# Weights of small blocks inverted by VectorE's reciprocal in place of ScalarE's Ln and Exp

## The chip, the cores and the metric

One core of a Trainium2 chip runs the whole program. The metric is device time in microseconds; the median of three runs of the kernel before is 5099.17 us (5098.44 to 5099.74). The profile was taken in one execution of its own, whose time stands in the table below. Engine names are those of the profile: PE (TensorE), DVE (VectorE), ACT (ScalarE), POOL (GpSimd), SP (SyncE, which issues the transfers).

## What is computed

Eight sequences of 512 tokens with 128 channels pass through two parts, all in float32. The first part, which the change touches, is one attention layer whose weights are not a softmax. For each of 16 heads of 8 channels the scores s = QK^T / sqrt(8) are taken over the causal positions, and a number lam is found for each row by four Newton steps so that the weights 1/(lam - s) sum to 1. Then the weights are taken once more, normalised, and applied to V:

```
lam = s_masked.max(-1) + 1.0
for _ in range(num_iter):                      # 4
    d = maximum(lam[..., None] - s, EPS)
    w = where(mask, 1 / d, 0.0)
    f = w.sum(-1) - 1.0
    fp = -where(mask, 1 / d**2, 0.0).sum(-1)
    lam = lam - f / fp
p = where(mask, 1 / maximum(lam[..., None] - s, EPS), 0.0)
o = (p / p.sum(-1, keepdims=True)) @ V
```

The second part is a stack of six layers with local attention and a feed-forward block each. Nothing in it is changed.

## The kernel before, in words

In the first part, a sequence (`b`) is cut into four row blocks of 128 queries (`rb` 0 to 3). Block `rb` sees W = 128 (rb + 1) keys. The 16 heads are taken in four quarters (`j` 0 to 3) of four heads; a quarter's scores for a block lie in one tile of 4W - 192 columns: 320, 832, 1344 and 1856 for rb 0 to 3. The columns hold four pieces, one for each 32 queries, with their own number of keys.

A loop over `work` takes two blocks at a time: (3, 0) of a sequence, then (2, 1) of it. Three such pairs are under way together. For the pair `nxt`, `scores` (L237) multiplies queries and keys on PE and stores the negated scores `ns` with their minimum through DVE (L253). For the pair `now`, `newton` (L283) makes one Newton step a round. For the pair `before`, which has its final lam, `attend_add` (L317) adds lam to the scores on POOL (L263, tile `da`), `attend_weigh` (L322) inverts the sum on ScalarE as Exp(-Ln(d)) in place (L324, L325), and `attend_sum` (L327) transposes the weights on PE (L338), masks them into SBUF on DVE (L341), multiplies by V on PE (L350) and copies the result out on DVE (L354). A loop of four rounds (`k`) inside does one quarter of `before` and of `nxt` and one Newton step of both blocks of `now` in each round.

A Newton step of a large block (W over 256) takes Ln with lam as bias for each piece (L297) and one Exp (L298) on ScalarE; for a small block POOL adds lam first (`add_lams`, L263, tile `df`) and one Ln (L293) and one Exp (L298) follow. DVE's statistics instruction (L300) gives means and spreads from which a chain of small DVE operations (L304 to L315, with a reciprocal of 16 columns in L313) makes the new lam. The next step of the same block waits for it.

The order of the instructions on each engine is set by a planner in the framework, which goes by its own cost of each operation, not by the source's order alone; each engine then works its queue off in that order. The tiles `da` rotate through three buffers; each of the score tiles `ns` of a block has a single buffer, so the next pair's scores wait until POOL has read the old ones. At the end of a pair `attend_end` (L362) divides by the sum of weights and applies the output weights, and once a sequence `normalized_T` (L88) and `project` (L190, with four copies in L198) prepare the next one. The second part has a reciprocal of 8 columns (L665) that is cited below.

Of the kernel before, what the change touches and what calls it, by code (L numbers as in the profile page):

```python
# [11 lines left out]
AF = mybir.ActivationFunctionType  # L12
# [4 lines left out]
P = 128  # L17
# [33 lines left out]
def tile_kernel(  # L51
# [18 lines left out]
    nc = tc.nc  # L70
# [38 lines left out]
    with ExitStack() as c1:  # L109
# [211 lines left out]

        def attend_weigh(t):  # L322
            d = t["d"]
            nc.scalar.activation(d, d, AF.Ln)  # L324
            nc.scalar.activation(d, d, AF.Exp, scale=-1.0)  # L325

        def attend_sum(t, d, j):  # L327

# [62 lines left out]
        for w in range(len(work) + 1):  # L391
            before, now, nxt = now, nxt, []
            if w + 1 < len(work):
                b, rbs = work[w + 1]
                nxt = [block(b, rb, proj) for rb in rbs]
            for t in now:
                first_lam(t)
            for k in range(NUM_ITER):
                if now:
                    add_lams(now[1])  # L400
                for u in range(2):
                    if before:
                        attend_add(before[u], k)
                    if nxt:
                        scores(nxt[u], k)
                    if now:
                        newton(now[u], k)
                    if ready:
                        attend_sum(*ready)
                        ready = None  # L410
                    if before:
                        attend_weigh(before[u])
                        ready = (before[u], before[u]["d"], k)
            if w + 2 < len(work) and work[w + 2][1][0] == 3:
                if ready:
                    attend_sum(*ready)
                    ready = None
                proj = project(work[w + 2][0])
# [412 lines left out]
    t = -1  # L831
# [100 lines left out]
```

## Time and profile before

| | |
|---|---|
| Time, median of 3 runs | 5099.17 us |
| Profiled execution, time / span | 5096.4 us / 5094.7 us |
| DVE busy | 4292.8 us (84%) |
| PE busy | 4212.5 us (83%) |
| ACT busy | 3544.0 us (70%) |
| POOL busy | 2982.7 us (59%) |
| First part (to about 1692 us): ACT, DVE, PE, POOL busy | 1492, 1404, 968, 751 us |
| L324 and L325, 320 columns, 32 each | 454 ns each |
| L324 and L325, 832 columns, 32 each | 884 and 886 ns each |

Busy time of an engine is the union of its instructions. Neighbouring instructions on DVE and ACT overlap by some tens of nanoseconds, since the next begins before the last one's result has been written; where an engine is never idle, the time from start to start is what an instruction costs. In the groups, a line gives the kernel line, engine, operation, the tile written and read, the shape, how often it ran, its busy time and mean duration, and the idle time of the engine before it with what ended it.

### The profile page before, as it was taken

How to read it: one execution, taken by the hardware profiler on the slowest of the kernel's cores; microseconds unless marked ns; L12 is line 12 of the kernel's file. 1: busy time of each engine (PE TensorE's matmuls, PEld its weight loads, DVE VectorE, ACT ScalarE, POOL GpSimd, SP SyncE). 2: the span in 40 equal slices, each digit the busy share in tenths (PEclk: the TensorE clock that was granted, in tenths of full speed). 3: DMA queues.
4: the chain of work that ended last, by engine and by line, in shares of the span. 5: the costliest groups of instructions: out<-in, count | busy, mean ns of one | idle time of the engine just before them, and what ended most of it. 6: DMA issues, size and time to landing. Idle time of an engine off the chain costs nothing.

```text
span 5094.7 us, 163374 instructions
## 1 busy us (share of the span) xinstructions
PE 4212.5 (83%) x67981; PEld 2491.9 (49%) x67981; DVE 4292.8 (84%) x11404; ACT 3544.0 (70%) x6314; POOL 2982.7 (59%) x3827
## 2 busy tenths in 40 slices
PE   4556566556554899999999999999999999999998
PEld 1223233223322555555555555565555555556555
DVE  7789888888887888888888888888888888888886
ACT  6889999999898566665666666656666566665664
POOL 2444434444445766666666666666666666666663
PEclk7667667667665999999999999999999999999999
DMA  0000000000001323232233222332223223233231
GB/s 9 1 5 1 5 5 1 5 3 3 3 1 26 72 58 73 61 76 64 56 73 72 65 67 58 74 75 56 69 58 81 68 55 72 61 76 73 62 75 47
DMA packets 273626, 237.61 MB, mean 47 GB/s; under 512 B 47056, under 2 KB 269048, under 8 KB 272888
## 3 DMA queue, kind: packets, MB, share of 16 engines
q1 hardware_dynamic: 272888, 227.16, 19.0%
q8 instruction: 538, 8.81, 0.8%
q14 instruction: 200, 1.64, 0.1%
HBM read 21.52 MB, written 4.19 MB: 5 GB/s over the span
## 4 chain that ended last, share of the span: by engine, by line
PE 43%; DVE 30%; ACT 19%; POOL 5%; issue 2%; SPq 0%; DMA 0%; ACTq 0%; POOLq 0%; DVEq 0%
PE m L552 9%; PE po L685 6%; DVE qr L568 5%; DVE stw L300 5%; DVE ss L558 5%; ACT d L297 5%; DVE qn L560 5%; PE pT L673 4%; PE acc L711 3%; ACT d L298 3%; PE ptq L619 3%; PE pv L588 3%; POOL da L263 2%; PE y L782 2%; PE gp L761 2%
## 5 line engine op out<-in xcount | busy, mean ns | idle before, releaser
L572 POOL TENSOR_TENSOR qn<-qn,qr 128x512 f32<-128x512 f32 x768 | 977.8, 1273 | 1047.4 <-DVE qr L568 827.2
L580 POOL TENSOR_TENSOR qn<-qn,ss 128x512 f32<-128x512 f32 x768 | 784.7, 1043 | 58.6 <-ACT ss L577 58.6
L558 DVE TENSOR_REDUCE ss<-sq 128x8 f32<-128x512 f32 x768 | 521.4, 679 | 351.0 <-ACT sq L557 351.0
L263 POOL TENSOR_TENSOR df<-ns,lam 128x32 f32<-128x32 f32 (+7 forms) x1024 | 396.9, 425 | 604.9 <-DVE lam L315 390.7
L552 PE MATMUL m<-wqkv,xs 128*128 128x512 f32 x1536 | 726.9, 596 | 2.0 <-ACT v L592 1.7
L297 ACT ACTIVATE d<-ns,lam 128x416 f32<-128x416 f32 (+7 forms) x1024 | 559.5, 615 | 64.9 <-DVE stw L300 27.5
L557 ACT ACTIVATE sq<-m 128x512 f32<-128x512 f32 x768 | 453.8, 597 | 187.4 <-PE m L552 184.7
L568 DVE TENSOR_TENSOR qr<-m,tab 128x256 f32<-128x256 f32 x1536 | 570.6, 412 | 0.0
L300 DVE BATCH_NORM_STATS2 stw<-d 128x6 f32<-128x416 f32 (+7 forms) x1024 | 514.6, 561 | 56.1 <-ACT d L298 55.7
L248 PE MATMUL s<-kn,qj 32*32 32x160 f32 (+15 forms) x4096 | 423.6, 491 | 151.4 <-DVE mn L253 136.6
L624 ACT COPY qT<-ptq 128x512 f32<-128x512 f32 x768 | 419.9, 579 | 175.1 <-PE ptq L619 175.1
L338 PE MATMUL dTp<-ident,da 128*128 128x128 f32 x1280 | 295.3, 371 | 294.8 <-issue 68.6
L560 DVE TENSOR_TENSOR qn<-m,tab 128x512 f32<-128x512 f32 x768 | 521.5, 679 | 0.0
L263 POOL TENSOR_TENSOR da<-ns,lam 128x416 f32<-128x416 f32 (+15 forms) x512 | 310.7, 639 | 319.3 <-PE dTp L338 252.5
L619 PEld LDWEIGHTS ptq<-ident,qn 128*128 128x128 f32 x3072 | 360.0, 141 | 210.4 <-issue 157.6
L685 PE MATMUL po<-v,prT 64*32 64x64 f32 x24576 | 389.3, 223 | 87.0 <-DVE pr L644 86.9
L588 PE MATMUL pv<-wqkv,xs 128*128 128x512 f32 x768 | 431.8, 644 | 4.9
L650 POOL TENSOR_TENSOR pr<-pr,nm 128x512 f32<-128x512 f32 x384 | 400.8, 1044 | 19.3 <-PE ptq L619 8.8
L711 PE MATMUL acc<-oT,wo 128*128 128x512 f32 x768 | 397.6, 599 | 14.9 <-ACT oT L705 14.9
L619 PE MATMUL ptq<-ident,qn 128*128 128x128 f32 x3072 | 399.3, 273 | 7.2 <-DVE qr L568 3.6
L338 PEld LDWEIGHTS dTp<-ident,da 128*128 128x128 f32 x1280 | 198.5, 186 | 422.3 <-issue 208.7
L685 PEld LDWEIGHTS po<-v,prT 64*32 64x32 f32 x24576 | 323.5, 105 | 166.5 <-DVE pr L644 136.5
(139 smaller groups left out, 8477.1 us busy)
## 6 DMA issues: line engine op xcount, KB each, us to landing
v<-v SPq DMA_DIRECT2D x1152, 128.0 KB
v<-v SPq DMA_DIRECT2D x384, 96.0 KB
v<-v SPq DMA_DIRECT2D x192, 64.0 KB
wqkv<-in_L_ffn_Wqkv_dram SPq DMA_DIRECT2D x24, 256.0 KB
wqkv<-in_L_ffn_Wqkv_dram SPq DMA_DIRECT2D x24, 128.0 KB
wo<-in_L_ffn_Wo_dram SPq DMA_DIRECT2D x12, 256.0 KB
xb<-in_L_attn_x_dram SPq DMA_DIRECT2D x8, 256.0 KB
x<-xb SPq DMA_DIRECT2D x8, 256.0 KB
```

Source lines behind the costliest of these rows:

```text
L263: nc.gpsimd.tensor_tensor(o, n, by.to_broadcast([P, keys(W, a)]), ALU.add)
L297: nc.scalar.activation(dv[a], nv[a], AF.Ln, bias=lam[:, c : c + 1])
L300: nc.vector.bn_stats(st[:, 4 * j + a].rearrange("p u k -> p (u k)"), dv[a])
L552: nc.tensor.matmul(m.rearrange("p h e -> p (h e)"), lhsT=lhsT, rhs=wqkv[:, t, :], start=True, stop=True,)
L558: nc.vector.tensor_reduce(ss[:, t, :], sq, axis=AX.X, op=ALU.add)
L560: nc.vector.tensor_tensor(qc, m, tab[:, 2 * t, c, :].unsqueeze(1).to_broadcast([P, HH, DHL]), ALU.mult)
L568: nc.vector.tensor_tensor(qr[:, :, u, :], mh[:, :, 1 - u, :], sw.unsqueeze(1).to_broadcast([P, HH, hd]), ALU.mult,)
L572: nc.gpsimd.tensor_tensor(qc, qc, qr.rearrange("p h u e -> p h (u e)"), ALU.add)
L580: nc.gpsimd.tensor_tensor(qc, qc, ss[:, t, :].unsqueeze(2).to_broadcast([P, HH, DHL]), ALU.mult)
L588: nc.tensor.matmul(pv, lhsT=lhsT, rhs=wqkv[:, 2, :], start=True, stop=True,)
L619: nc.tensor.transpose(pt[:, c * P : (c + 1) * P], g["qn"][t][:, c, 2 * p : 2 * p + 2, :].rearrange("p h e -> p (h e)"), ident,)
L685: nc.tensor.matmul(po[u * QB : (u + 1) * QB, e, c, :], lhsT=prT[rows, c, u * QB : (u + 1) * QB], rhs=g["v3"][rows, n, p * DHL : (p + 1) * ...
```

## The change

The blocks with W of at most 256 (rb 0 and 1) are inverted by one VectorE reciprocal of the whole quarter's tile, in place, instead of by ScalarE's Ln and Exp. Blocks 2 and 3 stay as they were, and so do all Newton steps. In the changed kernel's numbering the reciprocal is L325, and every later line moves down by three.

```
         def attend_weigh(t):
             d = t["d"]
-            nc.scalar.activation(d, d, AF.Ln)
-            nc.scalar.activation(d, d, AF.Exp, scale=-1.0)
+            if t["W"] <= 2 * P:
+                nc.vector.reciprocal(d, d)
+            else:
+                nc.scalar.activation(d, d, AF.Ln)
+                nc.scalar.activation(d, d, AF.Exp, scale=-1.0)
```

## The prediction

> **What bounds the kernel now.** I read the page's busy totals first, then busy time by stage, then groups by shape, and last the order of time on ScalarE and VectorE inside one iteration.
>
> ```profile
> span 5094.7 us, 163374 instructions
> PE 4212.5 (83%) x67981; PEld 2491.9 (49%) x67981; DVE 4292.8 (84%) x11404; ACT 3544.0 (70%) x6314; POOL 2982.7 (59%) x3827
> ...
> 629.00:830.00 201.00, 122.30 (x1040) 62.25 (x1040) 171.97 (x628) 184.78 (x268) 89.38 (x194) 0.67 0.01 4
> ...
> 0.00:1692.00 1692.00, 967.64 (x8370) 494.35 (x8370) 1404.33 (x5082) 1492.37 (x2161) 751.03 (x1642) 0.68 0.03 7
> ```
>
> The shares over the whole span mislead. The change is in the first part (to about 1692 us), and there ACT is busy 88% and DVE 83%; PE and POOL are at 57% and 44%. A window's line gives, after its length, PE, PEld, DVE, ACT and POOL. First_lam (L269) starts at 629.0 and 830.2: a batch takes 201.2 us. In the window 629 to 830 ACT is busy 184.8 us and DVE 172.0 us, so ACT leads with VectorE 13 us behind. Inside the batch:
>
> ```profile
> 659.20:684.30 25.10, 18.57 (x144) 7.78 (x143) 21.99 (x95) 22.81 (x32) 9.28 (x24) 0.67 0.00 1
> 684.30:707.50 23.20, 10.64 (x93) 5.91 (x93) 20.95 (x81) 22.79 (x32) 9.28 (x24) 0.61 0.00 1
> 727.50:773.80 46.30, 28.93 (x232) 15.58 (x232) 36.67 (x132) 36.89 (x56) 18.89 (x35) 0.65 0.05 12
> 773.80:797.20 23.40, 14.63 (x128) 7.27 (x129) 20.37 (x79) 22.29 (x31) 13.74 (x28) 0.69 0.00 1
> 797.20:818.20 21.00, 13.85 (x135) 6.18 (x137) 20.01 (x80) 21.00 (x32) 12.07 (x24) 0.69 0.00 1
> ```
>
> The first two windows are Newton iterations of row blocks 3 and 0, while blocks 2 and 1 of the batch before are weighed (call this stage A: its small block has 832 columns). The last two are iterations of blocks 2 and 1, with 3 and 0 being weighed (stage B, small block 320 columns). The middle one is the border, with the next batch's projection. An iteration is 21 to 25 us; ACT fills 91 to 100% of it, but DVE already fills 87 to 95%.
>
> **What goes.** ScalarE loses Ln (L324) and Exp (L325) of the small blocks, 32 of each at each size.
>
> ```profile
> 629.57 0.88 ACT L293 ACTIVATE df<-df 128x832 f32<-128x832 f32 x1
> 630.36 0.45 ACT L324 ACTIVATE da<-da 128x320 f32<-128x320 f32 x1
> 630.72 0.88 ACT L298 ACTIVATE df<-df 128x832 f32<-128x832 f32 x1
> ...
> L665 DVE RECIPROCAL rs<-rs 128x8 f32<-128x8 f32 x384 | 76.2, 199 | 8.3
> L313 DVE RECIPROCAL sw<-sw 128x16 f32<-128x16 f32 x128 | 30.5, 239 | 0.1
> ...
> 505.55 0.24 DVE L313 RECIPROCAL sw<-sw 128x16 f32<-128x16 f32 x1
> 505.71 0.20 DVE L300 BATCH_NORM_STATS2 stw<-df 128x6 f32<-128x96 f32 x1
> 505.83 0.17 DVE L314 TENSOR_TENSOR sw<-sw,sw 128x16 f32<-128x16 f32 x1
> 505.92 0.29 DVE L300 BATCH_NORM_STATS2 stw<-df 128x6 f32<-128x128 f32 x1
> ...
> 2015.21 0.20 DVE L665 RECIPROCAL rs<-rs 128x8 f32<-128x8 f32 x1
> 2015.33 0.64 DVE L693 TENSOR_TENSOR o<-po,rs 128x512 f32<-128x512 f32 x1
> ```
>
> Durations of neighbours overlap, so the cost on a busy engine is start to start: 832 columns take 630.36 - 629.57 = 0.79 us on ACT, 320 columns 630.72 - 630.36 = 0.36 us. ACT loses 2 x 0.79 = 1.58 us in each iteration of stage A and 0.72 us in each of stage B; over the kernel 32 x (1.58 + 0.72) = 73.6 us.
>
> **What comes.** VectorE gets 32 reciprocals of 320 and 32 of 832 columns. The trace has none that large, so I bound the slope. From 8 to 16 columns the duration goes from 199 to 239 ns, 5.0 ns a column; start to start it goes from 0.12 (2015.21 to 2015.33) to 0.16 us (505.55 to 505.71), also 5.0 at this rounding, and 4 where other instances show 0.15. I take 4.5 ns: 832 columns 0.155 + 816 x 4.5 ns = 3.83 us, 320 columns 0.155 + 304 x 4.5 ns = 1.52 us; 171 us over the kernel. Lower end: the slope of BATCH_NORM_STATS2 on this engine, (675 - 449) ns over 512 - 288 columns = 1.0 ns, giving 0.98 and 0.47 us. Upper end: L314 shows 0.09 us for 16 columns, so some 0.07 us is fixed; if a reciprocal had no more than 0.06 us fixed, 8 columns would cost 7.5 ns each: 6.3 and 2.5 us. The middle is nearest to the rows of the operation itself.
>
> The Trainium skill speaks against the change: "VectorE: DVE Perf Modes", section "First, the fixed hardware budget", says that Reciprocal is an iterative divide with a repeat count of 8. Read as 8 clocks of 0.96 GHz a column that is an estimate of 8.3 ns, about 7 us for 832 columns, and the sum would come out some 105 us higher than mine. The step between 8 and 16 columns, 0.04 us, is half of that, so the row decides.
>
> **What lies on the path.** In stage A the order of the changed kernel puts the 832 reciprocal on VectorE between the statistics (L300) of the third and of the fourth quarter of block 3. Behind it wait that fourth L300, the chain L304 to L315 and so lam; ScalarE's next four L297 wait for lam. Free VectorE time in such an iteration is 25.10 - 21.99 = 3.1 and 23.20 - 20.95 = 2.25 us, and 3.83 us must fit. Even with no wait left it grows by 0.7 and 1.6 us; ACT, at 22.8 - 1.58 = 21.2, is no longer the limit. Taking 1.15 for each of 4 iterations: +4.6 us a stage.
> At the border two 320 reciprocals come close together, among the normalization and the qj copies (L101, L198). VectorE is free 9.6 of 46.3 us there, but these stretches are a chain over PE, ACT and DVE; of 3.04 us I put half on the path (ends 0 and 3.0): +1.5 us. Each waits for POOL's L263 at the head of VectorE's queue; today it is ScalarE that waits so (4.14 us before L324 at 738.25).
> In stage B's last two iterations DVE comes to 20.37 + 1.52 = 21.9 of 23.4 and 20.01 + 1.52 = 21.5 of 21.0; ACT falls by 0.72. First: up to 0.7 gained; second: 0.5 lost; together -0.2 us.
> The buffers of da come free through the transposes L338, which follow the reciprocal; POOL's next add waits for them and L253 for POOL. The reciprocal ends about where the second ACT operation on da ended (it ran after the fourth Exp of block 3), so I cost this at nothing; if it is later, up to the 3.83 us per iteration that it takes. Order and issues on SP are as before, and no DMA is added. After the first part every queue has its old order.
> Sum: stage A runs 7 times with both kinds of work, the border 7 and stage B 8: 7 x 4.6 + 7 x 1.5 - 8 x 0.2 = +41 us. The last blocks are weighed with nothing beside them, where VectorE has room: 0. On the profiled execution's own 5096.4 us that makes 5137; it lies 2.8 us under the median of 5099.17, so I forecast 5140 us.
>
> **Rivals.**
> 1. Faster: VectorE's waits swallow everything and only ScalarE's relief counts. For it: ACT leads the batch by 13 us and DVE has 29 us free. Against: DVE would need 172.0 + 4 x 5.35 = 193.4 us of a batch whose ACT work falls to 175.6. The point of decision is the 832 reciprocal: below about 1.5 us (3.1 or 2.25 free, plus 1.58 that the iteration must shrink) stage A gets shorter, which takes a slope of 1.7 ns. At the lower end ACT leads and 7/8 of 73.6 us go: 5035 us; half of it 5067. Chance 0.16.
> 2. No change: part of VectorE's waits in stage A (L253 for POOL, 59.1 us in the first part) lie at the same point of the loop and are filled. Then stage A costs 0 and the border 1.5: about 5109. Chance 0.10.
> 3. Much slower: the upper slope, 6.3 and 2.5 us. Stage A +3.6 an iteration, border +2.5, stage B 0.5 gained and 1.5 lost, +1.0: 7 x 14.4 + 7 x 2.5 + 8 x 1.0 = +126, 5225 us. A later free da buffer gives the like. Chance 0.22.
> The forecast keeps 0.52.
>
> **Numbers.** The forecast's own range: slopes 4.0 to 5.2 ns move the 832 reciprocal by -0.4 to +0.6 us, so stage A by -11 to +17 us, and the border's ends by 10 each way: 5115 to 5170. Both signs hold chance, so the 8-in-10 range reaches down into rival 1 to 5085 and up into rival 3 to 5220. 0.2% (10 us) is about what a measurement of this kernel can tell from no change: faster 0.16, same 0.10, slower 0.74.
>
> **What would show it.** A reciprocal L325 of 832 columns near 3.8 us and one of 320 near 1.5; iterations of stage A about 1 us longer with DVE over 95% busy; ACT's idle time before L297, put down to DVE's lam or stw, up from the present 44.6 us for the 416-column form; ACT busy about 74 us (plus overlap, 86) less in the first part; the second part unchanged. I am wrong if the slope is not 4 to 5 ns, or if stage A keeps its length although DVE gets the work.

## The result, and the profile after

The changed kernel takes 5219.26 us (median of 4 runs, 5200.02 to 5226.27) against 5099.45 us (5098.44 to 5100.58) for the kernel before in the same comparison: a ratio of 1.0229, 95% interval 1.0217 to 1.0241. It is 120 us slower; the forecast was 41 us slower, with 5115 to 5170 us as its own range. The profiled execution took 5200.02 us (span 5198.3), 103.6 us more than the one before; where the time went is read from these two.

The page's busy totals, then windows of the changed kernel (length; PE, PEld, DVE, ACT, POOL; granted TensorE clock, DMA share, GB/s): the first and second part, one batch, and the first five Newton iterations of that batch (the first four are stage A). After them the two stages of the corresponding batch of the kernel before, which were not shown yet.

```profile
span 5198.3 us, 163365 instructions
PE 4282.5 (82%) x67981; PEld 2510.0 (48%) x67981; DVE 4499.5 (87%) x11468; ACT 3476.8 (67%) x6186; POOL 2983.5 (57%) x3827
```
```profile
0.00:1795.00 1795.00, 1036.62 (x8370) 511.54 (x8370) 1613.05 (x5146) 1425.01 (x2032) 750.19 (x1642) 0.65 0.03 7
1795.00:5198.30 3403.30, 3245.85 (x59612) 1998.50 (x59611) 2886.41 (x6323) 2051.81 (x4154) 2233.27 (x2186) 1.00 0.28 66
...
875.80:1088.30 212.50, 126.96 (x1041) 62.00 (x1041) 197.93 (x638) 176.62 (x253) 89.39 (x194) 0.66 0.01 3
875.80:991.10 115.30, 66.06 (x545) 33.06 (x545) 108.50 (x337) 89.73 (x128) 44.60 (x108) 0.65 0.00 1
991.10:1088.30 97.20, 60.91 (x496) 28.94 (x496) 89.43 (x302) 86.89 (x127) 44.78 (x88) 0.68 0.02 6
...
875.80:903.90 28.10, 17.42 (x159) 8.00 (x159) 24.86 (x74) 21.54 (x34) 11.24 (x28) 0.80 0.00 1
903.90:928.60 24.70, 13.93 (x125) 6.56 (x125) 24.25 (x75) 21.22 (x30) 9.28 (x24) 0.64 0.00 1
928.60:953.50 24.90, 14.25 (x125) 6.79 (x125) 24.36 (x75) 21.24 (x30) 9.28 (x24) 0.64 0.00 1
953.50:991.10 37.60, 20.46 (x136) 11.71 (x136) 35.02 (x119) 25.73 (x35) 14.80 (x32) 0.54 0.00 1
991.10:1018.80 27.70, 18.96 (x145) 8.49 (x149) 25.66 (x70) 24.23 (x38) 12.33 (x24) 0.69 0.07 20
```
```profile
833.00:929.30 96.30, 54.56 (x470) 27.32 (x470) 82.35 (x309) 90.70 (x132) 37.43 (x96) 0.68 0.00 1
929.30:1034.20 104.90, 65.01 (x570) 33.12 (x570) 89.73 (x322) 94.17 (x138) 51.98 (x99) 0.71 0.02 6
```

The second part kept its length (3403 us); all of the loss lies before it. The two engines changed places: ACT's work in the first part fell by 67 us (1492.4 to 1425.0), DVE's rose by 209 (1404.3 to 1613.1), and in the batch DVE now has 197.9 us of work and ACT 176.6. Stage A grew from 96.3 to 115.3 us, stage B shrank from 104.9 to 97.2. In stage A DVE had 13.95 us free (96.30 - 82.35); 26.15 us came (108.50 - 82.35), 6.8 us remain free, and the stage is 19.0 us longer. The four reciprocals are 21.4 us of the 26.15; the rest is for the most part masking (L341, now L344: 14.3 us in stage A before, 17.9 now) that stood in stage B before. So the two stages are to be read together: the batch is 11.3 us longer. The second and third iteration are full: DVE 24.25 of 24.70 us and 24.36 of 24.90.

The groups of the changed kernel, and one reciprocal among its neighbours on DVE (start, duration, instruction):

```profile
L325 DVE RECIPROCAL da<-da 128x832 f32<-128x832 f32 x32 | 170.9, 5342 | 2.5 <-POOL da L263 2.5
L325 DVE RECIPROCAL da<-da 128x320 f32<-128x320 f32 x32 | 68.5, 2139 | 0.0
L297 ACT ACTIVATE d<-ns,lam 128x416 f32<-128x416 f32 x128 | 80.8, 631 | 104.5 <-DVE lam L315 92.6 <-DVE lam L271 10.3 <-DVE stw L300 1.6
```
```profile
919.24 5.34 DVE L325 RECIPROCAL da<-da 128x832 f32<-128x832 f32 x1
924.50 1.62 DVE L300 BATCH_NORM_STATS2 stw<-d 128x6 f32<-128x416 f32 x3
```

Start to start 832 columns take 5.26 us, where 3.83 were forecast; the slope between the two sizes is (5342 - 2139) / 512 = 6.26 ns a column, where 4.5 was taken. Behind the reciprocal waits the fourth block of L300, and behind that lam: ACT's wait before L297 with 416 columns rose from 44.6 to 104.5 us.

The last 832-column reciprocal of a stage (968.97 to 974.3) shows the other end of the same wait. The timelines of DVE, POOL and ACT in the changed kernel (idle time before an instruction and its releaser in brackets):

```profile
978.14 0.16 DVE L315 SCALAR_TENSOR_TENSOR lam<-sw,lam 128x16 f32<-128x16 f32 x1
```
```profile
978.45 3.71 POOL L263 TENSOR_TENSOR da<-ns,lam 128x416 f32<-128x416 f32 x4 [16.81 <-DVE stw L300]
```
```profile
982.19 1.75 ACT L327 ACTIVATE da<-da 128x1856 f32<-128x1856 f32 x1 [9.97 <-POOL da L263]
...
987.63 1.75 ACT L327 ACTIVATE da<-da 128x1856 f32<-128x1856 f32 x1 [1.89 <-POOL da L263]
```

Block 3's final lam comes at 978 us; POOL's add reads it and can start only then (the bracket names the statistics that run beside L315), and ACT, whose queue now holds the Ln of the next weighing ahead of the next Newton step, waits in turn. Over the first part ACT's wait before this Ln of 1856 columns rose from 31.3 to 83.4 us.

By the first L297 of each iteration, the batch's 11.3 us (201.2 to 212.5) divide so: the first three iterations of stage A +2.2, the last of A with the first of B +9.7, the rest of B -0.6. Over the first part, whose last operation (L360 before, L363 now) ends 103.3 us later: start and first batch -4.5, the six batches after it +83.8, the last batch +3.8, and the end, from the start of the last Newton iteration, +20.2 us. That last piece had been forecast as 0.

### The profile page after: what moved, and what is told of

The parts are those of the page before. It is cut to its first block, busy times and chain, and to the rows that moved or that the text cites. A ratio compares the mean times of both kernels' runs of the same rounds, so it can differ in the third digit from the quotient of the medians.

```text
span 5198.3 us, 163365 instructions
## 1 busy us (share of the span) xinstructions
PE 4282.5 (82%) x67981; PEld 2510.0 (48%) x67981; DVE 4499.5 (87%) x11468; ACT 3476.8 (67%) x6186; POOL 2983.5 (57%) x3827
## 4 chain that ended last, share of the span: by engine, by line
PE 41%; DVE 35%; ACT 17%; issue 4%; POOL 3%; SPq 0%; DMA 0%; ACTq 0%; POOLq 0%; DVEq 0%
PE m L555 9%; DVE stw L300 7%; PE po L688 6%; DVE qr L571 5%; DVE ss L561 5%; ACT d L297 5%; DVE qn L563 4%; PE pT L676 4%; PE acc L714 3%; PE ptq L622 3%; ACT d L298 3%; PE pv L591 3%; PE gp L764 2%; PE y L785 2%; PE s L642 2%
## 5 line engine op out<-in xcount | busy, mean ns | idle before, releaser
L297 ACT ACTIVATE d<-ns,lam 128x416 f32<-128x416 f32 (+7 forms) x1024 | 559.8, 615 | 129.6 <-DVE lam L315 114.4
L341 PE MATMUL dTp<-ident,da 128*128 128x128 f32 x1280 | 324.1, 390 | 331.8 <-DVE dT L344 136.6
L263 POOL TENSOR_TENSOR da<-ns,lam 128x416 f32<-128x416 f32 (+15 forms) x512 | 310.7, 639 | 405.0 <-PE dTp L341 144.4
L300 DVE BATCH_NORM_STATS2 stw<-d 128x6 f32<-128x416 f32 (+7 forms) x1024 | 511.0, 559 | 35.4 <-ACT d L298 34.9
L248 PE MATMUL s<-kn,qj 32*32 32x288 f32 (+15 forms) x4096 | 441.6, 500 | 94.3 <-DVE mn L253 88.9
L341 PEld LDWEIGHTS dTp<-ident,da 128*128 128x128 f32 x1280 | 206.7, 194 | 512.7 <-issue 221.0
```

The lines of the kernel that those rows point to most:

```text
L263: nc.gpsimd.tensor_tensor(o, n, by.to_broadcast([P, keys(W, a)]), ALU.add)
L297: nc.scalar.activation(dv[a], nv[a], AF.Ln, bias=lam[:, c : c + 1])
L300: nc.vector.bn_stats(st[:, 4 * j + a].rearrange("p u k -> p (u k)"), dv[a])
```

## The experiments

Two theories go through the expectations. L: VectorE's own time decides; L1 means its summed time in the stage, L2 the place of the reciprocal ahead of the fourth statistics. O: the new order of the planner costs the time, not the reciprocal's length.

**Each size alone.**

```
             if t["W"] <= 2 * P:          # changed kernel
             if t["W"] == 2 * P:          # only832
             if t["W"] == P:              # only320
```

> Only row block 1 (832 columns) goes to VectorE; block 0 keeps Ln and Exp on ScalarE. Theory L (VectorE's own time decides: 5.27 us a reciprocal, against some 2.2 to 3.1 us that VectorE has free in a Newton iteration of blocks 3 and 0): those four iterations and the first stretch of the next stage stay as long as in the changed kernel, +2.2 and +4.0 us a batch, the rest of the batch as before: about +45 us, 5145. Theory O (the planner's new order costs, whatever the reciprocals take; above all the two Ln-Exp pairs of block 3's last weights that come ahead of the next stage's first Ln on ScalarE): the order changes with any such edit, so +70 us or more here too.

> Only row block 0 (320 columns) goes to VectorE; block 1 keeps Ln and Exp on ScalarE. Theory L: a reciprocal is 2.06 us start to start and the stage of blocks 2 and 1 has VectorE at 95% in one of its iterations: its last two iterations cost +5.1 us a batch in the changed kernel, eight times, +40 us, 5140; if the 832 ones caused part of that by coming late, +15. Theory O: as much as with both, +100.

With 832 alone 5229.57 us, ratio 1.0255 [1.0240, 1.0271]; with 320 alone 5112.99, ratio 1.0025 [1.0014, 1.0036]. The large reciprocals carry the loss. Theory L's forecast for 320 alone comes near (5115 us if part of its cost in the changed kernel came from the other size), but for 832 alone it missed: 5145 us were expected, from +6.2 us a batch, where the batch grew by 15.0 (216.2 against 201.2), and the "+70 us or more" of theory O came true. With the 320-column reciprocals added the kernel is faster again (5219 and 5201 us), although VectorE then has more work; whether ScalarE's further relief or the order does that was not separated. The windows of one batch, stage A and stage B, of the first kernel and then of the second:

```profile
882.80:999.50 116.70, 65.77 (x542) 33.93 (x543) 110.56 (x346) 92.05 (x132) 45.31 (x105) 0.62 0.00 1
999.50:1099.00 99.50, 60.06 (x500) 26.97 (x499) 81.78 (x290) 87.24 (x129) 44.08 (x90) 0.69 0.02 6
```
```profile
842.60:934.10 91.50, 54.79 (x467) 27.45 (x467) 80.30 (x297) 88.35 (x128) 35.75 (x95) 0.63 0.00 1
934.10:1047.40 113.30, 71.20 (x573) 35.58 (x573) 97.88 (x339) 94.53 (x133) 53.73 (x100) 0.65 0.02 6
```

With 832 alone stage A is 116.7 us long and DVE 95% busy, as in the full change. With 320 alone stage A is short again (91.5) and the reciprocals' time shows in stage B (DVE 89.73 to 97.88, the stage 104.9 to 113.3).

**Almost no time, and none, on VectorE.**

```
-                nc.vector.reciprocal(d, d)
+                nc.vector.tensor_tensor(d, d, d, ALU.max)    # cheap_op
+                pass                                         # relief_alone
```

> In place of the reciprocal VectorE takes the maximum of the tile with itself, in place: the weights of blocks 0 and 1 are left uninverted, the inversion is left out. About 1 ns a column: some 0.9 and 0.4 us. Theory L: VectorE has room for that, ScalarE's 9.2 us a batch are gained for the most part: 5040 to 5075. Theory O: the order is a new one here too, with ScalarE waiting for POOL at the border of the stages: not faster than before, 5100 or more.

> The inversion of blocks 0 and 1 is left out altogether: ScalarE loses its Ln and Exp, VectorE gets nothing. It prices what ScalarE's relief is worth by itself. Theory L: 9.2 us a batch of ScalarE's time, most of it on the path: 5030 to 5060. Theory O: the new order takes it back: 5090 or more.

Both leave the inversion out. cheap_op: 5077.61 us, ratio 0.9957 [0.9942, 0.9972]. relief_alone: 5059.99, ratio 0.9922 [0.9907, 0.9937]. The group lines of cheap_op:

```profile
L325 DVE TENSOR_TENSOR da<-da 128x832 f32<-128x832 f32 x32 | 34.1, 1066 | 3.5 <-POOL da L263 3.5
L325 DVE TENSOR_TENSOR da<-da 128x320 f32<-128x320 f32 x32 | 21.9, 684 | 2.6 <-POOL da L263 2.6
```

ScalarE's relief is worth 40.5 us (5100.49 - 5059.99), of the 73.6 us of work that it loses. An operation on the same tile with the same waits, at 1.07 us for 832 columns, leaves the kernel faster than before, and ACT's wait before L297 with 416 columns is 44.3 us there, as before the change (44.6). A transfer of the work to VectorE does not cost the time by itself, then. Length and place are not separated by this run, though: the planner gives the short operation other places. The reciprocal of 832 columns stands behind 12 of the 16 statistics (L300) of block 3 in every iteration of stage A, the short operation in the stage from 827 us behind 4, 8, 0 and 4. The next two runs change the place at full length. The first 56 us of VectorE's work (34.1 + 21.9) cost 17.6 us of time, the next 183 (239.4 - 56) cost 142, or 123 by the second comparison further down: the more of the free time is used up, the more of the work shows. The order is not quite free either. cheap_op's batches take two forms, 193.6 and 199.2 us long; in the longer ones the last iteration of stage A takes 30.9 us in place of 18.8, and more of the batch's work lies in that stage (359 of VectorE's instructions against 305). So some part of the border is the order's; it was not separated further.

**Same work, other places.** split4 cuts each reciprocal into the tile's four pieces, so that other work can go between them; late holds it in the source's order, where it stands on DVE behind the chain to lam.

```
-                nc.vector.reciprocal(d, d)
+                for c in pieces(d, t["W"]):                          # split4
+                    nc.vector.reciprocal(c, c)
+                tc.keep_in_program_order(nc.vector.reciprocal(d, d)) # late
```

> Each reciprocal is cut into the tile's four pieces (832 columns as 160, 192, 224 and 256), so VectorE's queue takes other work between them and the last piece no longer stands whole ahead of the fourth statistics of block 3. Theory L1 (VectorE's summed time decides: 24.2 of 24.7 us an iteration are filled): four fixed parts more, +0.3 us an iteration, 5215 to 5235. Theory L2 (the place decides: the 5.3 us stand ahead of the statistics that lam waits for, and of the last weights of block 3 at the border): ScalarE's wait for lam of 3.5 to 5.2 us and the 10 us wait at the border shrink, 5130 to 5175.

> The reciprocal is pinned behind what the source issues before it on VectorE, so it stands behind the chain that makes lam, not ahead of the fourth statistics; the planner orders the rest anew. L1: no shorter, 5190 to 5230. L2: 5130 to 5175.

split4: 5210.13 us, ratio 1.0214 [1.0197, 1.0231]. late: 5285.39, ratio 1.0361 [1.0346, 1.0377]. Neither repairs it: cut in pieces it lies between the two medians of the whole reciprocal (5219, and 5201 further down), and behind lam it loses another 66 us or more. L2 falls: both forecasts of 5130 to 5175 us fail. L1 comes near for split4 (5215 to 5235 expected). For late its 5190 to 5230 us fail too; the new order costs something that the summed time does not hold, and there is no control that has this pin without a reciprocal. Stage A of split4 is as long as with the whole reciprocal (115.5 us):

```profile
881.80:997.30 115.50, 64.23 (x510) 34.70 (x510) 106.53 (x344) 90.66 (x127) 43.77 (x105) 0.65 0.00 1
```

**Another order at the border.** The Ln of the large blocks is held to its place in the source's order, in the changed kernel and, as control, in the kernel before.

```
             else:
-                nc.scalar.activation(d, d, AF.Ln)
+                tc.keep_in_program_order(nc.scalar.activation(d, d, AF.Ln))
```

> The changed kernel, with the first ScalarE operation of the large blocks' inversion (Ln, L327, of 1344 and 1856 columns) held to its place in the source's order for the planner. The same arithmetic, only another order. Theory L (the time that VectorE needs decides): VectorE's work is the same, the stages with the 832-column reciprocal stay about 115 us long, and the time is within 10 us of the unpinned 5219 us. Theory O (at the border the new order puts the two pairs of 1856-column Ln and Exp ahead of the next stage's first L297, where they wait for POOL's da): the wait before L327, 83.4 us in all, falls to some 30 us, the last iteration of the stage falls from 37.6 us by about 4, and the time falls by some 30 us, to about 5190 us. If a pin of itself costs more than the order gives, as it did with the reciprocal, the control (pin_before) shows it.

> The control: the kernel before with the same operation (Ln of the large blocks, L324) held to its place in the source's order, and nothing else. What the pin itself does where no reciprocal stands on VectorE. If the order before is already the good one there: no change or a loss, 5099 us or more, by up to the 66 us that a pin of the reciprocal cost. If the pin is of use of itself: below 5090 us, and then a gain of pin_after is not a cure of what the change did. Theory L says nothing of it.

pin_after: 5259.19 us, ratio 1.0315 [1.0299, 1.0330]. pin_before: 5177.33, ratio 1.0153 [1.0136, 1.0170]. The pin did what it should at the border: the wait before the Ln of 1856 columns, 83.4 us, is gone. The time rose all the same, so both theories' forecasts of it (5219 and 5190 us) failed, and ACT's wait before L297 with 416 columns stayed at 103.5 us. Groups of pin_after, then its stages A and B, then those of pin_before:

```profile
L327 ACT ACTIVATE da<-da 128x1856 f32<-128x1856 f32 x32 | 55.5, 1736 | 0.0
L297 ACT ACTIVATE d<-ns,lam 128x416 f32<-128x416 f32 x128 | 81.0, 633 | 103.5 <-DVE lam L315 84.6 <-DVE lam L271 10.3 <-DVE stw L300 8.6
```
```profile
890.60:1007.20 116.60, 68.67 (x531) 37.12 (x529) 109.67 (x339) 85.79 (x124) 41.07 (x101) 0.59 0.00 1
1007.20:1112.90 105.70, 68.47 (x514) 33.41 (x512) 89.52 (x300) 91.47 (x129) 48.45 (x95) 0.63 0.02 6
```
```profile
868.50:968.10 99.60, 62.43 (x467) 29.15 (x468) 83.77 (x312) 90.62 (x131) 36.92 (x96) 0.60 0.00 1
968.10:1080.70 112.60, 71.50 (x574) 35.02 (x574) 88.44 (x320) 95.24 (x140) 52.55 (x99) 0.68 0.02 6
```

With the pin on both sides, too, the reciprocals make stage A 17.0 us longer and stage B 6.9 shorter (19.0 and 7.7 without the pin), and the kernel 81.9 us slower. So the loss does not need the wait at POOL: that was where the lack of VectorE's time appeared, not its cause. The pin costs the kernel before 79 us. Since 81.9 is less than the 120 and 103 us without the pin, some 20 to 40 us of those may be the order's and the clock's; this was not separated.

**Again, for the spread.** The changed kernel itself (after_again).

> The changed kernel itself once more, for a second profile. Its runs so far lie between 5200 and 5226 us, while the kernel before stays within 2 us. If TensorE's granted clock is what differs: the stages with the 832-column reciprocal again differ by several us among themselves, the long ones start with an iteration in which the clock stands at about 0.50, and which stages these are is not the same as in the first profile (there the one at 654 us). If the spread comes from elsewhere: the same stages are long in both profiles, with the same clock.

5200.68 us (5198.69 to 5216.84), ratio 1.0207 [1.0190, 1.0224]. The profile shows what differs: the first iteration of a stage A normally takes about 28 us, but 35.7 where the granted clock stays at 0.50 (a half-clock iteration below). In the first profile that happened once (the stage at 654 us), in this one three times (868, 1090 and 1524 us). Windows of 28 us from the start of two stages, then two pieces of the half-clock iteration:

```profile
655.40:683.40 28.00, 18.53 (x159) 8.59 (x159) 24.39 (x69) 21.60 (x33) 11.24 (x28) 0.74 0.01 1
868.50:896.50 28.00, 26.18 (x155) 10.08 (x155) 17.24 (x53) 20.59 (x33) 11.28 (x28) 0.50 0.00 1
...
875.50:882.50 7.00, 7.00 (x32) 2.96 (x32) 3.48 (x11) 5.26 (x9) 3.07 (x5) 0.50 0.01 2
882.50:889.50 7.00, 7.00 (x29) 1.90 (x28) 4.26 (x13) 3.78 (x6) 0.00 (x0) 0.50 0.00 0
```

At half clock TensorE is the bound there (26.2 of 28 us) and DVE waits for it (17.2 us of work in place of 24.4). Each such iteration costs some 7 us. That answers for most of the 16.8 us between the two profiled spans (two more of them, 14.4 us). For the timed runs, 5198.69 to 5226.27 us over both comparisons, it is likely: they have no profile, but the mean granted clock of each is on record and goes with its time (0.876 to 0.878 in the four runs of 5199 to 5202 us, 0.873 and 0.874 in the three of 5217 to 5219, 0.868 at 5226).

**The end of the first part.** The four 832-column inversions that follow the last Newton step go back to ScalarE; the other 28 stay on VectorE.

```
-            if t["W"] <= 2 * P:
+            if t["W"] <= 2 * P and beside:      # beside: the blocks whose Newton step runs in this round
```

> The changed kernel, except that the last four operations of 832 columns, which run after the last Newton step with no other Newton work beside them, stay on ScalarE as Ln and Exp. 28 of the 32 reciprocals of 832 columns and all 32 of 320 stay on VectorE. Theory T (the end of the first part, which the prediction costed at nothing, pays 20 us of its own, because each of these four reciprocals lies on the chain from POOL's add over the inversion, the transposes and VectorE's masking to the free buffer of the next add): the stretch from the last iteration to the last operation of the first part falls from 85.2 us to about 65 us, as before the change, and the time by 17 to 22 us, to about 5198 us against 5219 and 5201 us in the two comparisons so far. Its rival (the stretch is long because the changed order left more work for it, wherever the inversion runs): it stays above 78 us, and the time falls by less than 8 us. TensorE's clock moves single stages by some 7 us in this kernel, so the stretch in the profile decides, and the total only with it.

5179.05 us (5169.69 to 5195.94), ratio 1.0155 [1.0141, 1.0169]. In its profile the half-clock iterations fall in the same three stages as in after_again, so these two compare directly. The stretch from the start of the last Newton iteration to the end of the first part, of tail_on_acte, then of after_again, then of the kernel before:

```profile
1706.70:1768.40 61.70, 39.13 (x352) 25.05 (x353) 48.93 (x147) 42.25 (x53) 32.03 (x59) 0.75 0.20 55
```
```profile
1706.50:1791.40 84.90, 45.98 (x352) 29.77 (x353) 69.31 (x152) 35.40 (x45) 32.05 (x59) 0.66 0.16 40
```
```profile
1606.80:1671.80 65.00, 40.85 (x386) 26.69 (x387) 46.57 (x144) 42.24 (x56) 34.24 (x65) 0.71 0.24 62
```

84.9 us become 61.7, and the span falls by 20.9 us (5215.1 to 5194.2). The median is 22 us under that of after_again and 40 under the first one, lower than expected; the stretch decides, and theory T holds. The chain is seen on DVE and POOL of the changed kernel, in the last two quarters:

```profile
1741.90 5.35 DVE L325 RECIPROCAL da<-da 128x832 f32<-128x832 f32 x1 [1.26 <-POOL da L263]
1748.50 0.42 DVE L344 TENSOR_TENSOR dT<-dTp,seen 128x256 f32<-128x256 f32 x1 [0.45 <-PE dTp L341]
...
1754.72 5.35 DVE L325 RECIPROCAL da<-da 128x832 f32<-128x832 f32 x1 [1.26 <-POOL da L263]
```
```profile
1748.55 2.86 POOL L263 TENSOR_TENSOR da<-ns,lam 128x288 f32<-128x288 f32 x4 [6.68 <-PE dTp L341]
1752.68 2.01 POOL L263 TENSOR_TENSOR da<-ns,lam 128x160 f32<-128x160 f32 x4 [1.27 <-PE dTp L341]
```

A quarter takes 12.8 us (1741.90 to 1754.72). POOL waits for a da buffer, which comes free through the transposes; these wait for the reciprocal, and while it runs DVE can't mask the transposed weights of the other block. Before, ScalarE inverted while DVE masked, and a quarter took 6.1 us (Ln of 832 columns at 1653.33 and at 1659.42).

**Another engine.** The inversion as a power of -1 on POOL.

```
+        neg = k1.tile([P, 8 * P - 6 * Q], F32, name="neg")
+        nc.gpsimd.memset(neg, -1.0)
...
-                nc.vector.reciprocal(d, d)
+                nc.gpsimd.tensor_tensor(d, d, neg[:, 0 : 4 * t["W"] - 6 * Q], ALU.pow)
```

> The inversion of blocks 0 and 1 goes to POOL as a power of -1 (tensor against a tile of -1), neither ScalarE nor VectorE has it. POOL is 44% busy in the first part. If a column costs POOL no more than its add (about 2 ns: 1.7 and 0.7 us), this comes near the run with the inversion left out: 5060 to 5090. If it costs 10 ns or more a column (8 us for 832), POOL's adds for the Newton steps come late: 5150 or more.

10451.28 us, ratio 2.0491 [2.0461, 2.0522], far beyond the second case of the forecast; the groups of this kernel:

```profile
L327 POOL TENSOR_TENSOR da<-da,neg 128x832 f32<-128x832 f32 x32 | 4259.5, 133109 | 2.0
L327 POOL TENSOR_TENSOR da<-da,neg 128x320 f32<-128x320 f32 x32 | 1647.1, 51471 | 1.9
```

**The price by itself.** The kernel before, with reciprocals of eight sizes at its very start, three of each.

```
+        rb_t = k1.tile([P, 1024], F32, name="rb_t")
+        nc.gpsimd.memset(rb_t, 3.0)
+        for rb_n in (8, 16, 32, 64, 128, 256, 512, 1024):
+            for _ in range(3):
+                nc.vector.reciprocal(rb_t[:, 0:rb_n], rb_t[:, 0:rb_n])
```

> The kernel before, with reciprocals of 8 to 1024 columns, three each, on a tile of its own ahead of everything. It prices the size that I had to guess from 8 and 16 columns: 6.25 ns a column and about 0.14 us fixed by the changed kernel's two sizes; 16 columns 0.24, 128 columns 0.94, 512 columns 3.3, 1024 columns 6.5 us. If the cost has a step, 64 and 128 columns fall off that line.

A single run, 5121.94 us. Five of the groups:

```profile
L132 DVE RECIPROCAL rb_t<-rb_t 128x1024 f32<-128x1024 f32 x3 | 19.6, 6540 | 0.0
L132 DVE RECIPROCAL rb_t<-rb_t 128x512 f32<-128x512 f32 x3 | 10.0, 3342 | 0.0
L132 DVE RECIPROCAL rb_t<-rb_t 128x64 f32<-128x64 f32 x3 | 1.6, 541 | 0.0
L132 DVE RECIPROCAL rb_t<-rb_t 128x16 f32<-128x16 f32 x3 | 0.8, 253 | 0.1
L132 DVE RECIPROCAL rb_t<-rb_t 128x8 f32<-128x8 f32 x3 | 0.6, 203 | 2.0 <-POOL rb_t L129 2.0
```

A straight line: (6540 - 3342) / 512 = 6.25 ns a column, and with the same neighbours (253 - 203) / 8 = 6.25 ns as well, above some 0.15 us. The steps between small sizes were fit to give the slope; the two rows that the prediction took were not, since 199 and 239 ns come from different lines with different neighbours.

## Why the prediction was right and wrong

**The price of the reciprocal** is the first step that failed, a mis-sized term: "832 columns 0.155 + 816 x 4.5 ns = 3.83 us, 320 columns 0.155 + 304 x 4.5 ns = 1.52 us". Measured were 5.26 and 2.06 us (992.51 to 994.57 on DVE). The mechanism into which the term went held in the main. With the right size the prediction's own sum is: stage A 1.15 + 1.43 = 2.58 us an iteration, 10.3 a stage; half of 4.12 us at the border, 2.06; stage B 0.35; 7 x 10.3 + 7 x 2.06 + 8 x 0.35 = +89 us in place of +41. The two rows differ by 40 ns over 8 columns, and an error of 10 ns in that difference is 1.25 ns a column and a microsecond at 832. The true value lies above the forecast's 4.0 to 5.2 ns and below the upper end of 7.5. That end came from a fixed part of 0.06 us, which was right (5.26 - 832 x 6.25 ns), and from 0.12 us at 8 columns, a figure with two decimals: 0.01 us less there gives 6.25.

Here a page of the Trainium skill spoke against the number taken, "VectorE: DVE Perf Modes", section "First, the fixed hardware budget", with a repeat count of 8. Read as 8 clocks a column (8.3 ns, an estimate) it was too high, as the rows' 4.5 was too low; the measured 6.25 ns lies between them.

**The end of the first part** is the second: "The last blocks are weighed with nothing beside them, where VectorE has room: 0." It cost 20.2 us. VectorE has room there on average (46.6 of 65.0 us busy before), but the work is a chain, and in this chain an operation costs its length although its engine is free at other times: four times 5.26 - 1.58 are 14.7 of the 20.2 us. That the rest is the masking, which now stands in line with the inversion on one engine, fits the trace, but was not separated. The same step underlies "so I cost this at nothing" for the da buffers: at the end it failed. In the batches nothing speaks against it (POOL's wait before the adds to da for the transposes fell, from 252.5 to 144.4 us over the first part), though POOL's whole wait before these adds rose from 319.3 to 405.0 us, the new part of it mostly until DVE's statistics and lam.

**The sum of the rest.** Without the end the profiled loss is 83.1 us; without the one iteration at half clock (7.2 us) some 76, against 89 from the corrected terms. The total is near, its places are not, so the agreement is in part luck. "Even with no wait left it grows by 0.7 and 1.6 us": at the right size these are 2.1 and 3.0 us for the second and third iteration, measured -0.4 and +2.0. "+1.5 us" for the border (with the +1.15 of the iteration ahead of it): measured +9.7. An iteration that has no time to spare on VectorE leaves work to the next (the last of stage A has 119 of VectorE's instructions, 47 before), and the account is settled where the stage ends and block 3's last lam is due. That the 320-column reciprocals wait for POOL at the head of VectorE's queue did not come either (0.0 us in the group above). "-0.2 us" for stage B's last two: they took 5.1 us more (21.8 + 26.8 against 20.9 + 22.6), which the one ahead of them, 5.7 us shorter, made up.

**What held.** Slower, with VectorE as the new bound of stage A, and the reciprocal of 832 columns between the third and the fourth quarter's statistics; the waits before L297 with 416 columns up from 44.6 us (104.5), put down to DVE's lam; ACT's work down, by 67 us where 74 to 86 were named; the second part unchanged. The point from which rival 1 decides, 832 columns in about 1.5 us, does not contradict cheap_op, where 1.07 us give a faster kernel; nothing between 1.07 and 5.26 us was run, so the point itself is not shown. Its 5035 us are out of reach: with no operation at all it is 5060. A likely reason is that VectorE (171.7 us of work in a batch of 194.6) is then nearly as full as ScalarE (176.4). Rival 2 falls (A's waits were not simply filled). The result, 5219 and 5201 us in two comparisons, lies nearest to rival 3's 5225, but that is luck in good part: its slope of 7.5 ns is 1.25 too high, and the end of the first part and TensorE's clock, which it does not have, make up the difference.

None of the versions that compute the same result beats the kernel before. Moving this work to VectorE pays only at a price per column that the reciprocal does not have: 5.26 us against 1.58 us for both of ScalarE's operations.

## What to carry to other kernels

When the trace has an operation only at tiny sizes, two rows from different places do not give a slope; compare rows with the same neighbours, and where there are none, let both ends of the price stand in the forecast's own range, since here 1.75 ns a column were 48 us of the forecast, nearly half of the profiled loss. An engine that is 85% busy, as VectorE was in stage A, has little to give: sum its work stage by stage, and look for the excess where the stage's last result is due as well as where the operation stands. Price the end of a part on its own, as a chain: here, with nothing beside it, operations that are 14.7 us longer in all cost 20.2 us.

## What was not expected of the hardware

- The power on POOL takes (133109 - 51471) / 512 = 159 ns a column, 25 times VectorE's reciprocal.
- TensorE's granted clock stayed at 0.50 through a whole iteration while TensorE was busy 7.00 of 7.00 us in two windows in a row. The Trainium skill, "TensorE: Matmul & The Clock Gate", section "What's actually happening", gives two levels, half and full, and says that a busy stretch of about 3.4 us lifts the gate. The levels agree (0.50 here, 1.00 in the second part); that 14 us of a busy TensorE lift it does not agree with these windows, although a profile's busy share is no proof that the array works without a gap. Why some stages get the clock and others don't stays open. It costs about 7 us each time; the kernel before shows 0.75 in that place in each of six stages, so it may pay this nowhere.
